# Late loads of x1 into the places of z2, and a reordered start and end of the second map

## The chip, the cores and the metric

The kernel runs on one core of a Trainium2 chip, all in fp32. The metric is the device time of one execution in microseconds; the figure quoted is the median of three. The engines in what follows are TensorE (PE, with its weight loads PEld), VectorE (DVE), ScalarE (ACT), GpSimd (POOL) and SyncE (SP), which here issues the loads and most stores by DMA; the stores of the output are issued by ACT.

## The reference

Two layers over x of shape (16, 1024, 256), each a residual around a normalised and rectified input. Cut to what matters:

```python
h = relu(layernorm(x))
# layer 0: graph weights from channel means, 4-head attention
g = relu(einsum('bcn,bnm->bcm', h_T, adj * A_s) * para)
x = x + softmax(q @ k.T * scale) @ v           # q from g, k and v from h @ kv_w
# layer 1
h = relu(layernorm(x))
agg = einsum('nm,bmd->bnd', A_hat, h)          # A_hat: adj + I, normalised by degree
z1 = agg @ W1.T + b1                           # 512 channels
z1 = relu(batchnorm(z1))                       # statistics over all 16 * 1024 rows
z2 = batchnorm(z1 @ W2.T + b2)                 # 256 channels, statistics over all rows
x = x + z2
```

The two batch norms need statistics over all rows, so the program has three stages: everything up to z1 for all batches, z2 for all batches, and the output for all batches.

## The kernel before

**Stage 1** (lines 171 to 1222) runs over 16 batches: layer norm, graph product, attention, layer norm, aggregation and first map. The result of layer 0, called x1, goes to device memory (`leave`, L943), and so does z1 in 32 tiles of 512 rows (two per batch). PSUM has three pools here: `ps_s` with three tiles of two banks, `ps_o` and `ps_t` with one bank each. They are all closed with the stage.

For the last two batches, 14 and 15, there is no further attention to hide behind. The code at L1176 to L1222 gives the aggregation of batch 14 (`linear1_all`, `linear1`, `linear1_seven`) three hooks, `first`, `second` and `third`, in which the second half of batch 15's attention output is scaled and added (`left[3]` to `left[5]`) and batch 15's second layer norm is made: `Norm.stats` (DVE, one `bn_stats` per 128 rows), `Norm.invert` (an add on DVE, then a power on POOL, L257), `Norm.shifts` (DVE, L263), `Norm.relu` (ACT, L278, eight rows of 256). `third` also transposes W2 through one tile of `ps_o` and one of `ps_t`. After the hook, `linear1_seven` adds two products to a tile of z1 (DVE, L864 and L865); then batch 15's aggregation starts (PE, L703). At its end (`very_last`) the last parts of z1 are made on PE (L891), evacuated by ACT (L900), their statistics taken by DVE, and the first rectified tiles of z1, zs[0,0] and zs[1,0], made by ACT (`relu_on`, L152).

**Stage 2** (L1241 to L1456) has its order written out by hand for all five engines. Tiles 0 and 1 (batch 0) are multiplied plainly (`plain`, `product`, L1255). The fourteen pairs of tiles of batches 1 to 14 are multiplied with seven products in place of eight (`Pair`: `m1` to `m7`, L1317; sums on DVE, L1307 to L1313). In one pass of the loop the products of one pair interleave with the rectification (ACT, L152) of the next pair and the copies `keep` (ACT, L1328) and adds `out` (DVE, L1331) that carry PSUM into `z2`. `z2` is one SBUF tile of [128, 2, 15, 1024]: two halves of the channels, 15 batches, 1024 rows, and is kept until stage 3. Tiles 30 and 31 (batch 15) come after the loop (L1476 to L1505): their results stay in four PSUM banks (`last`). PSUM pools are `ps_x` with four banks (the running sum `self.x` of a pair; later `last`) and `ps_z` with four (`begun`, `m2`, `m7`), which closes after the loop and makes room for `ps_out`, two tiles of two banks.

The last product, tile 31 for channel half 1, is split into two of 256 columns, so that the statistics of the first (L1496) run beside the second. `gather` makes the earlier tiles' statistics into triples; `bn2.invert` and `bn2.affine` end them.

**Stage 3** (L1538 to L1579) runs over the batches. PE transposes the scaled z2 into `ps_out` (L1534); `finish` scales z2 in place, two batches ahead, on ACT (L1514) or DVE (L1516); DVE adds the transposed result to x1 (L1573) in x1's tile; ACT issues the store (L1574).

x1 comes back from memory in half batches of 512 KB (`load_x1`, L1238). `AHEAD` is 10: batch 0 is loaded before the last pair, batches 1 to 6 and 9 in it and behind it, batches 7 and 8 into the places of the last z1 tiles, and batch b + 10 at the end of pass b of stage 3. These last six batches take tiles of the pool `io` (15 places of 4 KB per partition), in which the places are those of batches whose output has been stored. In front of batches 1 to 6 in SP's order stands the fetch of the last z1 tile, zs[31,2], into one of four places; the place before belonged to the last pair's b21, read by `m2`.

Of the kernel before, what the change touches and what calls it, by code (L numbers as in the profile page):

```python
# [29 lines left out]
def fast_path(  # L30
# [135 lines left out]
    def relu(t, f2):  # L166
        zs[t, f2] = fetch(t, f2)
        relu_on(zs[t, f2], f2)


    with ExitStack() as stage:
        ps_s = stage.enter_context(tc.tile_pool(name="fps_s", bufs=3, space=PSUM))
        ps_o = stage.enter_context(tc.tile_pool(name="fps_o", bufs=1, space=PSUM))
        ps_t = stage.enter_context(tc.tile_pool(name="fps_t", bufs=1, space=PSUM))
        big = stage.enter_context(tc.tile_pool(name="fbig", bufs=1))
# [870 lines left out]
        with tc.manual_schedule(engines={ENG.PE, ENG.Activation, ENG.DVE, ENG.Pool, ENG.SP}):  # L1046
# [73 lines left out]
            for b in range(B):  # L1120
# [55 lines left out]
                else:  # L1176
# [3 lines left out]
                    def first():  # L1180
                        norm.stats(0, 4)
                        left[3]()
                        left[4]()

                    def second():
                        pass

                    def third():
                        left[5]()
                        norm.stats(4, NC)  # L1190
                        norm.invert()
                        for n, (pool, tag) in enumerate(((ps_o, "o"), (ps_t, "t"))):
# [9 lines left out]
                            )  # L1202
                        norm.relu(0, NC)
                        leave(b)
# [20 lines left out]
    with ExitStack() as stage:  # L1225
# [5 lines left out]

        def load_x1(b, homes=None):

            xts[b] = []
            for h in range(NH):
                pool, tag, bufs = (homes or HOMES)[h]
                t = pool.tile([P, NC // NH, C], F32, tag=tag, name=f"f_x1t_{b}_{h}", bufs=bufs)
                nc.sync.dma_start(t, x1_d[b].rearrange("(p h i) d -> p h i d", h=NH, p=P)[:, h])  # L1238
                xts[b].append(t)

        st2 = big.tile([P, CC, TT, 6], F32, tag="st2", name="f_st2")  # L1241
        with tc.manual_schedule(engines={ENG.PE, ENG.Activation, ENG.DVE, ENG.Pool, ENG.SP}):
            bn1.affine(FC - 2, FC)

            z2 = big.tile([P, CC, B - 1, N], F32, tag="z2", name="f_z2")
            ps_x = stage.enter_context(tc.tile_pool(name="fps_x", bufs=4, space=PSUM))
            zps = ExitStack()
# [144 lines left out]
            pairs = {p: Pair(p) for p in SEVEN}  # L1392
            begun = {t: [bank(f"f_z2ps_{t}_{c}") for c in range(CC)] for t in (1, 0)}
            first = pairs[SEVEN[0]]
# [14 lines left out]
            first.m1()  # L1409
            first.keep(0, 0)  # L1410
            for p in SEVEN:
                now, soon = pairs[p], pairs.get(p + 1)
# [20 lines left out]
                if soon:  # L1433
                    soon.relu(1, 1)
                    soon.relu(1, 0)
                else:
                    relu_all(TT - 1)
                now.m5()
                now.keep(1, 1)
                if soon:  # L1440
                    soon.sums13()
                    soon.m1()
                    soon.keep(0, 0)
                now.out(1)
                now.m3()
# [13 lines left out]
            ps_out = stage.enter_context(tc.tile_pool(name="fps_out", bufs=2, space=PSUM))  # L1459
            last = {}  # L1460

            triples = big.tile([P, 6, 3], F32, tag="triples", name="f_triples")
            SPLIT = TT // 2
# [12 lines left out]
            for c in range(CC):  # L1476
                for t in range(TT - 2, TT):
                    ps = bank(f"f_z2ps_{t}_{c}", ps_x)
                    last[t % 2, c] = ps
                    if c + 1 < CC or t + 1 < TT:  # L1480
                        product(ps, t, c, 0)
                        product(ps, t, c, 2)
                        nc.vector.bn_stats(st2[:, c, t, :], ps)
                        continue
                    gather(1, SPLIT, TT - 1)
                    for k in range(2):
                        at = slice(256 * k, 256 * (k + 1))
                        for f in range(FC):
                            nc.tensor.matmul(
                                ps[:, at],  # L1490
                                w2T[:, f, ts(c, P)],
                                zs[t, f - f % 2][:, f % 2, at],
                                start=(f == 0),
                                stop=(f == FC - 1),
                            )
                        nc.vector.bn_stats(  # L1496
                            triples[:, 2 + 2 * k : 4 + 2 * k, :].rearrange("p k s -> p (k s)"),
                            ps[:, at],
                        )
                bn2.invert(  # L1500
                    c,
                    c + 1,
                    None if c + 1 < CC else triples.rearrange("p k s -> p (k s)"),
                )
                bn2.affine(c, c + 1)  # L1505
# [32 lines left out]
            for b in range(B):  # L1538
# [19 lines left out]
                else:  # L1558
                    for h in range(NH):
                        for c in range(CC):  # L1560
                            turn_out(b, h, c, outs[h])
                soon = [(b + 2, c) for c in range(CC) if (b + 2, c) not in ready]
                soon = soon if b + 2 < B else []
# [13 lines left out]
                finish_soon(False)  # L1577
                if b + AHEAD < B:
                    load_x1(b + AHEAD)  # L1579

# [513 lines left out]
```

## Time and profile before

| | us |
|---|---|
| median of three runs | 2431.84 (2431.0 to 2432.97) |
| the profiled execution | 2431.68 |
| its span, first to last instruction | 2429.8 |
| PE busy | 2387.0 (98%) |
| DVE busy | 1781.9 (73%) |
| ACT busy | 1325.6 (55%) |
| POOL busy | 308.2 (13%) |
| stage 2's first product starts | 2163.9 |
| first transpose into the output | 2362.9 |
| last store issued | 2420.6 |

Times on the profile's axis count from the first instruction, so the span ends at 2429.8. A busy share is an average over stages: PE's 98% hides that PE is at 100% in nearly all of stages 1 and 2 and about 60% in stage 3. The chain of work that ended last gives PE 96% and DMA 2% of the span.

### The profile page before, as it was taken

To read this page: it belongs to the slowest core of one execution; us is meant where nothing else is said; L and a number is where in the kernel's file an instruction comes from. 1 tells how busy PE (TensorE), PEld (TensorE's weight loads), DVE (VectorE), ACT (ScalarE), POOL (GpSimd) and SP (SyncE) were. 2 spreads that over 40 slices of the span, in tenths; PEclk is the share of its full clock that TensorE was granted. 3 is DMA by queue.
4 is the path that set the end of the run, shared out by engine and by line. 5 is a ranking of instruction groups with operands and counts; after the bars stand their busy time and mean duration, and the time that the engine had idled before them with its cause. 6 is when DMAs were issued, how large, how long until landed. Compare 5 with 4: busy or idle time off the path is not lost.

```text
span 2429.8 us, 24669 instructions
## 1 busy us (share of the span) xinstructions
PE 2387.0 (98%) x8042; PEld 1053.3 (43%) x8042; DVE 1781.9 (73%) x2441; ACT 1325.6 (55%) x1932; POOL 308.2 (13%) x546
## 2 busy tenths in 40 slices
PE   8999999999999999999999999999999999999995
PEld 4453444434343434444343434344443434444444
DVE  6878677685949586776859595867768596757766
ACT  6845555464636455554546364545545465346653
POOL 2030202020020302020201103020202010000000
PEclk9999999999999999999999999999999999999997
DMA  5041414232331415142323224141423212355569
GB/s 186 9 140 61 152 61 126 87 91 73 116 94 60 144 61 152 61 126 87 102 67 114 91 63 142 61 151 61 126 87 110 67 61 76 110 209 178 174 225 379
DMA packets 176634, 275.77 MB, mean 113 GB/s; under 512 B 37872, under 2 KB 121328, under 8 KB 176496
## 3 DMA queue, kind: packets, MB, share of 16 engines
q1 hardware_dynamic: 156336, 241.55, 30.6%
q0 software_dynamic: 15552, 15.77, 2.5%
q10 hardware_dynamic: 4608, 16.78, 1.7%
q8 instruction: 66, 1.08, 0.2%
q14 instruction: 72, 0.59, 0.1%
HBM read 169.35 MB, written 71.10 MB: 99 GB/s over the span
## 4 chain that ended last, share of the span: by engine, by line
PE 96%; DMA 2%; DVE 1%; ACT 0%; issue 0%; SPq 0%; POOL 0%; DVEq 0%; ACTq 0%; POOLq 0%
PE f_s L506 19%; PE f_o L547 18%; PE f_gps L398 18%; PE f_aps L703 16%; PE f_zps L809 6%; PE f_vps L423 5%; PE f_zx L1317 4%; PE f_zm L1317 3%; PE f_kpsx L467 2%; PE f_kps L467 1%; DMA out_dram<-f_x1t 1%; PE f_z2ps L1255 1%; PE f_zps L891 1%; PE f_kps L440 1%; PE f_zps3a L809 0%; PE f_zps3b L809 0%
## 5 line engine op out<-in xcount | busy, mean ns | idle before, releaser
L514 ACT ACTIVATE f_p<-f_s 128x1024 f32<-128x1024 f32 x512 | 477.3, 1048 | 150.2 <-PE f_s L506 150.1
L523 DVE TENSOR_TENSOR f_acc<-f_acc,f_p 128x1024 f32<-128x1024 f32 x384 | 470.5, 1225 | 41.1 <-ACT f_w L345 0.5
L506 PE MATMUL f_s<-f_qT,f_kT 64*128 64x512 f32 x2048 | 456.8, 596 | 0.0
L547 PE MATMUL f_o<-f_p,f_v 128*64 128x512 f32 x2048 | 453.6, 595 | 0.0
L398 PE MATMUL f_gps<-f_w,f_h_a 128*128 128x512 f32 x1024 | 444.7, 594 | 0.3 <-DVE f_w L336 0.3
L368 POOL DMA_DIRECT2D f_hT<-f_hQ x480 | 235.8, 499 | 1220.0 <-PE f_gps L398 1170.8
L506 PEld LDWEIGHTS f_s<-f_qT,f_kT 64*128 64x128 f32 x2048 | 190.8, 186 | 263.5 <-ACT f_p L514 117.0
L398 PEld LDWEIGHTS f_gps<-f_w,f_h_a 128*128 128x128 f32 x1024 | 192.8, 190 | 247.0 <-issue 230.7
L547 PEld LDWEIGHTS f_o<-f_p,f_v 128*64 128x64 f32 x2048 | 141.4, 137 | 304.3 <-issue 254.4
L349 DVE SCALAR_TENSOR_TENSOR f_w<-f_w,f_adj 128x1024 f32<-128x1024 f32 x127 | 153.9, 1212 | 38.8 <-ACT f_w L348 38.8
L345 ACT ACTIVATE f_w<-f_row,f_col 128x1024 f32<-128x1024 f32 x127 | 147.0, 1158 | 31.2 <-DMA f_row<-frow 30.2
L278 ACT ACTIVATE f_h_b<-f_x,f_shift_b,f_rstd_b 128x256 f32<-128x256 f32 x128 | 67.8, 594 | 160.9 <-DVE f_shift_b L263 160.9
L348 ACT ACTIVATE f_w<-f_w 128x1024 f32<-128x1024 f32 x127 | 134.3, 1058 | 4.0
L703 PE MATMUL f_aps<-f_ahatT,f_hs 128*128 128x512 f32 x256 | 115.1, 592 | 0.0
L703 PE MATMUL f_aps<-f_ahatT,f_h_b 128*128 128x512 f32 x256 | 112.7, 593 | 0.8 <-DVE f_z L865 0.8
L423 PE MATMUL f_vps<-f_kvw,f_hT 128*128 128x256 f32 x512 | 113.4, 379 | 0.0
L703 PE MATMUL f_aps<-f_t,f_hs 128*128 128x512 f32 x256 | 112.5, 592 | 0.0
L278 ACT ACTIVATE f_h_a<-f_x,f_shift_a,f_rstd_a 128x256 f32<-128x256 f32 x126 | 73.8, 587 | 63.5 <-DVE f_shift_a L263 63.4
L423 PEld LDWEIGHTS f_vps<-f_kvw,f_hT 128*128 128x128 f32 x512 | 97.2, 190 | 20.3 <-issue 7.4
L520 DVE TENSOR_TENSOR f_acc<-f_p,f_p 128x1024 f32<-128x1024 f32 x64 | 76.3, 1192 | 15.3 <-ACT f_p L514 15.3
L589 ACT COPY f_recs<-f_rec 32x32 f32<-32x32 f32 x128 | 31.5, 246 | 98.7 <-DVE f_rec L581 97.5
L574 ACT COPY f_parts<-f_red 32x64 f32<-32x64 f32 x128 | 39.1, 306 | 78.5 <-DVE f_red L539 77.4
(227 smaller groups left out, 2709.7 us busy)
## 6 DMA issues: line engine op xcount, KB each, us to landing
f_t<-ft SPq DMA_DIRECT2D x84, 512.0 KB, 6.9
fz<-f_z SPq DMA_DIRECT2D x64, 512.0 KB, 9.6
f_x<-in_x_dram SPq DMA_DIRECT2D x31, 1024.0 KB, 8.1
f_zb<-fz SPq DMA_DIRECT2D x42, 512.0 KB, 4.3
f_para<-in_L_gnn_para_dram SPq DMA_DIRECT2D x32, 512.0 KB, 4.5
f_att<-f_oT SPq DMA_DIRECT2D x512, 32.0 KB, 1.9
fx<-f_x SPq DMA_DIRECT2D x16, 1024.0 KB, 6.3
f_x1t<-fx SPq DMA_DIRECT2D x32, 512.0 KB, 7.3
```

What stands on the lines that cost most here:

```text
L345: nc.scalar.activation(w, rows[b], AF.Abs, bias=cols[b][:, c : c + 1], scale=0.5 / C)
L349: nc.vector.scalar_tensor_tensor(w, w, 1.0, adj_t[c], ALU.subtract, ALU.mult)
L368: queue.dma_start(to[ts(k, 32), ts(a, 32 * NC)], t[ts(a, 32), k].rearrange("i c r -> i (c r)"),)
L398: nc.tensor.matmul(gps[d][:, ts(g, 512)], hs[b][:, c, ts(d, P)], w[:, ts(g, 512)], start=(c == 0), stop=(c == NC - 1),)
L423: nc.tensor.matmul(ps[:, i, :], hT[e][:, ts(c4 + i, P)], kvw_t[:, e, C : 2 * C], start=(e == 0), stop=(e == CC - 1),)
L506: nc.tensor.matmul(ps[:, e, :], kT[rows_e, pair, ts(m, P)], qT[rows_e, pair, ts(g, 512)], start=True, stop=True,)
L514: nc.scalar.activation(p, ps, AF.Exp)
L523: nc.vector.tensor_add(acc_of[s], acc_of[s], p)
L547: nc.tensor.matmul(o_of[s][e * HD : (e + 1) * HD, :], v[:, m, ts(2 * pair + e, HD)], p[:, e, :], start=(m == 0), stop=(m == NC - 1),)
L703: nc.tensor.matmul(ps, left[:, m, :], right(m), start=not more and m == 0, stop=(m == KH - 1), skip_group_check=more,)
L809: nc.tensor.matmul(ps[i], left[:, ts(i, P)], right, start=not more, stop=True, skip_group_check=more,)
L1317: nc.tensor.matmul(ps, left[:, m, :], right[:, m, :], start=start and m == 0, stop=(m == 1), skip_group_check=not start,)
```

## The change

It has five parts.

1. The pools `ps_o` and `ps_t` are opened ahead of stage 1 and stay open to the end. `ps_x` has two banks in place of four. Tiles 0's two products (`begun[0]`) go to one tile of each of these pools (`aside`), and later the products of tiles 30 and 31 for channel half 0 (`ends`).
2. Batch 15's second layer norm is made in two halves: statistics and power of rows 0 to 3 in `first`, their shifts and rectification in `second`, and the other half in `third`.
3. In the last pass over the pairs, the rectification of tile 31 moves from in front of `m5` to behind `keep(1, 1)`, and the product of tile 30 for channel half 0 follows it, in front of `m3`.
4. The last product is no longer split; its statistics are one `bn_stats` over 512 columns, and `triples` has four entries in place of six.
5. The loads of batches 10 to 15 go into `z2[:, h, b, :]`, the places of batch b's two channel halves, and are issued behind the transposes of batch b in place of the end of pass b.

```diff
+    ps_o = ctx.enter_context(tc.tile_pool(name="fps_o", bufs=1, space=PSUM))
+    ps_t = ctx.enter_context(tc.tile_pool(name="fps_t", bufs=1, space=PSUM))
     with ExitStack() as stage:
         ps_s = stage.enter_context(tc.tile_pool(name="fps_s", bufs=3, space=PSUM))
-        ps_o = stage.enter_context(tc.tile_pool(name="fps_o", bufs=1, space=PSUM))
-        ps_t = stage.enter_context(tc.tile_pool(name="fps_t", bufs=1, space=PSUM))
...
                     def first():
                         norm.stats(0, 4)
+                        norm.invert(0, 4)
                         left[3]()
                         left[4]()
                     def second():
-                        pass
+                        norm.shifts(0, 4)
+                        norm.relu(0, 4, False)
                     def third():
                         left[5]()
                         norm.stats(4, NC)
-                        norm.invert()
+                        norm.invert(4, NC)
...
-                        norm.relu(0, NC)
+                        norm.shifts(4, NC)
+                        norm.relu(4, NC, False)
                         leave(b)
...
-        def load_x1(b, homes=None):
+        def load_x1(b, homes=None, places=None):
...
+                if places is not None:
+                    t = places[h].rearrange("p (i d) -> p i d", d=C)
+                else:
...
-            ps_x = stage.enter_context(tc.tile_pool(name="fps_x", bufs=4, space=PSUM))
+            ps_x = stage.enter_context(tc.tile_pool(name="fps_x", bufs=2, space=PSUM))
...
-            begun = {t: [bank(f"f_z2ps_{t}_{c}") for c in range(CC)] for t in (1, 0)}
+            def aside(name):
+                return [
+                    ps_o.tile([P, 512], F32, tag="o", name=f"{name}_0"),
+                    ps_t.tile([P, 512], F32, tag="t", name=f"{name}_1"),
+                ]
+            begun = {0: aside("f_z2ps_0"), 1: [bank(f"f_z2ps_1_{c}") for c in range(CC)]}
...
+            def last_product(t, c, ps):
+                last[t % 2, c] = ps
+                for f2 in range(0, FC, 2):
+                    product(ps, t, c, f2)
...
-                else:
-                    relu_all(TT - 1)
                 now.m5()
                 now.keep(1, 1)
                 if soon:
                     soon.sums13()
                     soon.m1()
                     soon.keep(0, 0)
+                else:
+                    relu_all(TT - 1)
+                    ends = aside("f_z2ps_end")
+                    last_product(TT - 2, 0, ends[0])
                 now.out(1)
                 now.m3()
...
-            triples = big.tile([P, 6, 3], F32, tag="triples", name="f_triples")
+            triples = big.tile([P, 4, 3], F32, tag="triples", name="f_triples")
...
-                    ps = bank(f"f_z2ps_{t}_{c}", ps_x)
-                    last[t % 2, c] = ps
+                    if (t % 2, c) not in last:
+                        last_product(t, c, ends[1] if c == 0 else bank(f"f_z2ps_{t}_1", ps_x))
                     if c + 1 < CC or t + 1 < TT:
-                        product(ps, t, c, 0)
-                        product(ps, t, c, 2)
-                        nc.vector.bn_stats(st2[:, c, t, :], ps)
+                        nc.vector.bn_stats(st2[:, c, t, :], last[t % 2, c])
                         continue
                     gather(1, SPLIT, TT - 1)
-                    for k in range(2):
...
+                    nc.vector.bn_stats(
+                        triples[:, 2:4, :].rearrange("p k s -> p (k s)"), last[t % 2, c]
+                    )
...
                             turn_out(b, h, c, outs[h])
+                if b + AHEAD < B:
+                    load_x1(b + AHEAD, places=[z2[:, h, b, :] for h in range(NH)])
...
                 finish_soon(False)
-                if b + AHEAD < B:
-                    load_x1(b + AHEAD)
```

More of the change, by code (lines that the diff above doesn't have):

```diff
@@ L1230, in fast_path @@
         HOMES = [(io, "x1", None)] * NH
-        def load_x1(b, homes=None):
+        def load_x1(b, homes=None, places=None):
             xts[b] = []
             for h in range(NH):
-                pool, tag, bufs = (homes or HOMES)[h]
-                t = pool.tile([P, NC // NH, C], F32, tag=tag, name=f"f_x1t_{b}_{h}", bufs=bufs)
+                if places is not None:
+                    t = places[h].rearrange("p (i d) -> p i d", d=C)
+                else:
+                    pool, tag, bufs = (homes or HOMES)[h]
+                    t = pool.tile(
+                        [P, NC // NH, C], F32, tag=tag, name=f"f_x1t_{b}_{h}", bufs=bufs
+                    )
                 nc.sync.dma_start(t, x1_d[b].rearrange("(p h i) d -> p h i d", h=NH, p=P)[:, h])
@@ L1410, in fast_path @@
             first.keep(0, 0)
+            last = {}
+            def last_product(t, c, ps):
+                last[t % 2, c] = ps
+                for f2 in range(0, FC, 2):
+                    product(ps, t, c, f2)
             for p in SEVEN:
@@ L1459, in fast_path @@
             ps_out = stage.enter_context(tc.tile_pool(name="fps_out", bufs=2, space=PSUM))
-            last = {}
-            triples = big.tile([P, 6, 3], F32, tag="triples", name="f_triples")
+            triples = big.tile([P, 4, 3], F32, tag="triples", name="f_triples")
             SPLIT = TT // 2
@@ L1477, in fast_path @@
                 for t in range(TT - 2, TT):
-                    ps = bank(f"f_z2ps_{t}_{c}", ps_x)
-                    last[t % 2, c] = ps
+                    if (t % 2, c) not in last:
+                        last_product(t, c, ends[1] if c == 0 else bank(f"f_z2ps_{t}_1", ps_x))
                     if c + 1 < CC or t + 1 < TT:
-                        product(ps, t, c, 0)
-                        product(ps, t, c, 2)
-                        nc.vector.bn_stats(st2[:, c, t, :], ps)
+                        nc.vector.bn_stats(st2[:, c, t, :], last[t % 2, c])
                         continue
                     gather(1, SPLIT, TT - 1)
-                    for k in range(2):
[L1487 to L1499, printed above, removed]
+                    nc.vector.bn_stats(
+                        triples[:, 2:4, :].rearrange("p k s -> p (k s)"), last[t % 2, c]
+                    )
                 bn2.invert(
```

## The prediction

> **What bounds the kernel now.** I read the table of stretches first, because the page's slices are too coarse for the last 100 us, where most edits lie. Columns: stretch, length, busy us of PE, weight loads, DVE, ACT and POOL with instruction counts, granted TensorE clock, DMA share, GB/s.
>
> ```profile
> 2332.00:2338.00 6.00, 6.00 (x15) 2.66 (x14) 4.89 (x7) 4.00 (x6) 0.00 (x0) 1.00 0.01 3
> 2338.00:2342.00 4.00, 4.00 (x10) 1.71 (x9) 1.98 (x4) 2.00 (x3) 0.00 (x0) 1.00 0.67 179
> 2342.00:2362.00 20.00, 17.71 (x47) 8.57 (x46) 8.88 (x21) 6.09 (x8) 0.55 (x1) 1.00 1.01 396
> 2362.00:2374.00 12.00, 8.87 (x64) 7.03 (x64) 9.48 (x15) 6.68 (x6) 0.55 (x1) 1.00 0.77 270
> 2374.00:2404.00 30.00, 18.17 (x112) 15.00 (x111) 18.93 (x18) 12.67 (x11) 0.00 (x0) 0.78 1.02 413
> 2404.00:2424.00 20.00, 13.08 (x89) 11.08 (x88) 15.47 (x14) 7.97 (x9) 0.00 (x0) 0.84 1.03 417
> ```
>
> Two regimes. Until about 2342 PE has no gap worth the name (the stretches before are at 100% too). From 2342 to 2424 the DMA engines are full at 396 to 417 GB/s, except from 2362 to 2374, at 270. So the tail ends when about 33 MB (30 half loads of x1, one of z1, 32 half stores, 0.52 MB each) have been moved, counted from 2338, when the first of them is issued. Only three things shorten this kernel: an earlier 2338, fewer holes after it, or an earlier end of PE's stages, which is an earlier 2338.
>
> Next the waits. Of the DMA queue on SP from 2366 to 2400, and of PE's longest pauses around the last linear stage (2110 to 2125, 2160 to 2178) and the last pair (2336 to 2368). Columns: waiter, releaser, total us, times, longest.
>
> ```profile
> SPq L1238 <- DMA out_dram<-f_x1t: 30.5, 12, 7.2
> ```
>
> ```profile
> DVE f_shift_b L263 <- POOL f_rstd_b L257: 1.8, 1, 1.8
> ...
> PE f_aps L703 <- DVE f_z L865: 0.8, 1, 0.8
> ```
>
> ```profile
> PE f_z2ps L1255 <- ACT f_z L900: 1.4, 1, 1.4
> ```
>
> ```profile
> PE f_zx L1317 <- ACT f_z L1328: 1.8, 1, 1.8
> ACT f_z L152 <- DMA f_z<-fz: 1.1, 1, 1.1
> ```
>
> All twelve late loads of x1 wait for stores to land; PE pauses for 0.83, 1.40 and 1.77 us. Last, POOL's powers by shape:
>
> ```profile
> L257 POOL TENSOR_TENSOR f_rstd_b<-f_var_b,f_mhalf 128x8 f32<-128x8 f32 x16 | 27.5, 1721 | 149.1 <-DVE f_var_b L256 149.1
> L257 POOL TENSOR_TENSOR f_rstd_a<-f_var_a,f_mhalf 128x4 f32<-128x4 f32 x2 | 2.1, 1055 | 2.3 <-DVE f_var_a L256 2.3
> ```
>
> **What the Trainium skill says.** "DMA: Bandwidth & Descriptors", section "Bandwidth", puts the ceiling of the core's port fabric at 435 GB/s; the trace's plateau of 413 to 417 GB/s is 95% of it, so I treat the plateau as a limit that reordering can't raise. The same page, "Queues, rings and completion order", says each DMA engine takes turns between the queues that have work. The trace agrees: from 2384 to 2400 the stores' queue moved 3.54 MB and the loads' 3.16 MB. "TensorE: Matmul & The Clock Gate", Part 1, says a PE with too little to do falls to half clock; the trace shows 0.78 granted in 2374 to 2404. "PSUM — Partial Sum Buffer", "Specifications", gives 8 banks of 512 fp32 values, which is how I count the pools below.
>
> **The change, part by part.** Its own profile: span 2429.8, time 2431.68, 1.9 around it; the median shown is 2431.84, 0.16 above. I work with differences and take them from the median.
>
> *Half norms of the last batch.* The 8-column power, its statistics' tail and eight ACT rows become two halves. In the third hook DVE stands at L263 for POOL (power 2120.05 to 2121.69), with L864 and L865 (1.22 us each) behind it in order; L865 frees the PSUM tile for which PE waits, from 2123.66 to 2124.49. With four columns the power takes 1.05 instead of 1.64: L865 ends 0.59 sooner, PE starts at 2123.90. Gain 0.59 of 0.83. Added: one variance add and one shift on DVE (0.17 each) in the hooks before, under waits of 2.73 and 3.4 us; one power on a POOL that is otherwise idle; four of ACT's eight relus (8 took 4.04) now at 2101.4 to 2103.4, before L755, for which ACT stands idle until 2103.94. If that cover failed, L755 would slip by at most 2 us, and DVE and PE slots behind it with it. Bounds for the part: 0.2 to 0.83; I take 0.59.
>
> *PSUM pools o and t live on; the first z2 products go there.* PE ended f_zps at 2162.50 and began f_z2ps at 2163.90, released by ACT's last evacuation L900 (2163.17 to 2163.86). By the banks, 2 (o, t) + 2 (ps_x) + 4 (ps_z) = 8, the new homes have had no user since about 2129, so only the relu of zs[0,0] is left, which ended at 2162.60. Gain 1.26. The next wait is for the second relus: they depend on ACT and DVE, which do not move; PE would want zs[0,2] at 2169.5 and ACT had it at 2169.42. In the first pair ACT is busy until 2178.5; keep(0,0) would then end near 2179.1, and m6 wants it at 2179.8; keep(0,1) near 2182.5 and m5 at 2183.2. Tight by 0.6 us, but covered. ps_x with 2 buffers holds the two f_zx alive at a time. Bounds: 0 (if the wait is of another tile) to 1.4; I take 1.26.
>
> Both gains are PE's and pass through the thirteen following pairs (2177.7 to 2338, PE 100%) to SP: the fetch of zs[31,2], for which PE's m2 frees a slot at 2337.9, heads SP's queue of loads. So 2338 comes 1.85 us earlier.
>
> *The last pair.* relu_all(31) moves behind keep(1,1), and a product of tile 30 (four matmuls, 3.43 us) in front of m3. The 1.77 us pause goes, since keep(1,1) no longer stands behind two relus that await a DMA landing at 2342.67; the unsplit last product drops the 0.52 pause at L1489 and 0.2 of split cost, for 0.27 more of statistics (0.70 for 0.43). Relative to m2: m5 ends 2342.9, then 3.43 + 1.72 + 1.72 + 10.30 gives 2360.05 for PE, last statistics 2360.3 to 2361.0 against 2363.54: 2.5 us sooner. Behind it, unchanged, 1.5 us of aggregation, scaling, transposes, add: the first store issues at 2365.1 instead of 2367.66. m3 and m4 come 1.7 us later in PE's time, and they free two of the loads' places, at 2348.1 and 2349.9; those loads were issued at 2349.41 and 2351.97, so nothing slips. By itself all this moves no DMA byte: it counts in the next sum.
>
> *Loads into z2 behind the transposes.* Twelve half loads no longer wait for a store to land (7 to 10 us after its issue) but for eight transposes (1.1 us). SP has nothing queued behind them. The hole: 12 us at 270 and the rest at 381 until 2378 lacks, against 418, (418−270)×12 + (418−381)×4 = 1.92 MB, or 4.6 us. In the new order the loads of batches 7 and 8 are issued at 2355.2 to 2360.3 (they were at 2357.2, 2358.9, 2362.3, 2363.1, behind PE's reads of z), which keeps the engines full to about 2366; stores from 2365.1 and loads from 2366.3 show about 1.2 us later. Hole left: about 0.3. Gain 4.3; bounds 2.5 (the new loads gain nothing, only stores and four loads come sooner) to 4.6.
>
> Does the tail then stay DMA bound? Loads and stores share until about 2397, then some 19 stores are left, 19 × 1.25 = 24 us. DVE needs per batch two adds of 1.22 and on average 0.4 of scaling, 2.85 us, ACT about 2.5, against 2.5 for the DMA; but by then the chain is up to eight stores ahead. Eight batches × 2.85 from 2397 end near 2420 at worst, the DMA near 2422. Covered, by 2 us.
>
> Sum: 0.59 + 1.26 + 4.3 = 6.15 us. 2431.84 − 6.15 = **2425.7 us**, −0.25%.
>
> **Rivals.**
> A. The new places bring nothing: the load's wait turns out to be for more than the batch's transposes (the scaling of later batches in the same z2, or a landing as before). For it: z2 is one tile. Against: reads, copies and statistics of z2 overlap in the trace at 2343 to 2352. Then 1.85 + about 2 = 3.9 us: 2428.0.
> B. The wait at 2163.9 only changes its name (relu, or ACT in the first pair, where cover is 0.6 us). For it: ACT is 8.87 of 10 us busy at 2170 to 2180. Then 0.59 + 4.3: 2426.95, on the bound.
> C. Loads ahead of stores starve the end. Loads taken early leave more stores than now for the last stretch; if loads got well over the half that they get now, the stores would begin in earnest only at 2381 (12 × 1.25 after 2366), PE at half clock, where 32 transposes took 6.33 us (2402.2), 3.2 per batch, and the add of 1.22 not overlapped: 4.4 × 14 batches = 62, end 2443; plus 3 of landing, 2.5 of close and 1.9 around the span, less 1.85 and 0.3: about 2448. It decides once a batch takes over 3.6 us from 2381 on (50 us in place of 62). Against it: the equal shares above, and four stores in flight per side.
>
> **How the numbers follow.** 0.2%, 4.9 us, is about what a measurement of this kernel can tell from none: 2426.98. Forecast 62%, A 17%, B 13%, C 8%. The forecast's own range, with the three gains at 0.2 to 0.83, 0.6 to 1.4 and 3.4 to 4.6 (their lower ends are B and A), is 2425.0 to 2427.6; A and B stretch the upper end, repeat spread (1 us either way) both: 2424.0 to 2428.6. Faster: the forecast less a tenth (56%), half of B and a fifth of A: 66%. Same: 26%. Slower: C, 8%.
>
> **What would show it.** Right: PE's pause before f_aps near 0.2, before f_z2ps under 0.2, none before m3; DMA at or above 395 GB/s in every stretch from first load to last store; the late loads issued 1 us behind transposes, all by about 2390 instead of 2398. Wrong: a new pause of PE in the first pair (B), SP waiting for landings (A), or a DMA share under 0.95 after the last load (C).

## The result and the profile after

The changed kernel takes 2425.47 us (median of ten runs, 2424.30 to 2427.18) against 2432.19 us for the kernel before (median of ten), a ratio of 0.9972 with a 95% interval of 0.9964 to 0.9980: 6.7 us, or 0.28%, faster. The forecast was 2425.7. The profiled execution has a span of 2424.1 us and a time of 2425.91, 5.77 below the profiled execution of before.

Every line number from 170 on has moved: L257 is now L258, L703 is L704, L1238 is L1247, L1255 is L1264, L1317 is L1326, L1328 is L1337, L1514 and L1516 are L1526 and L1528, L1534 is L1546, L1574 is L1588.

First the table of stretches, with the same columns as before (stretch, length, busy us and instructions of PE, weight loads, DVE, ACT and POOL, granted clock, DMA share, GB/s):

```profile
2330.00:2336.00 6.00, 6.00 (x15) 2.66 (x14) 4.89 (x7) 3.96 (x6) 0.00 (x0) 1.00 0.01 3
2336.00:2340.00 4.00, 4.00 (x10) 1.71 (x9) 1.16 (x2) 0.59 (x1) 0.00 (x0) 1.00 0.94 228
2340.00:2360.00 20.00, 18.27 (x49) 8.35 (x47) 10.25 (x28) 8.96 (x11) 1.10 (x2) 1.00 1.02 407
2360.00:2372.00 12.00, 9.85 (x56) 8.83 (x57) 9.35 (x10) 6.80 (x7) 0.00 (x0) 0.72 1.01 377
2372.00:2384.00 12.00, 6.23 (x48) 5.14 (x48) 9.41 (x9) 2.05 (x2) 0.00 (x0) 1.00 1.03 416
2384.00:2396.00 12.00, 8.48 (x48) 7.24 (x48) 6.12 (x6) 7.55 (x7) 0.00 (x0) 0.72 1.03 398
2396.00:2402.00 6.00, 4.26 (x32) 3.43 (x32) 5.83 (x7) 4.68 (x5) 0.00 (x0) 1.00 1.03 421
```

The stretch around the first stores, 270 GB/s before, is at 377. A smaller hole is left in it, and there is a new dip, 398, from 2384 to 2396. Next the waits of SP's queue from 2358 to 2400 (waiter, releaser, total us, times, longest):

```profile
SPq L1247 <- PE f_outps L1546: 7.0, 5, 3.2
SPq L1247 <- DMA out_dram<-f_x1t: 5.5, 2, 3.0
SPq L1247 <- DMA f_z<-fx: 5.1, 3, 2.1
```

Before, all twelve late loads waited for a landing of a store, 30.5 us in all. Now five waits end with the transposes (L1546); two are still put down to a store and three to an earlier late load, for a reason that the last section gives. Then PE's timeline at the three places where it used to pause (start, duration, instruction, count; a pause would stand in brackets at the end of the line):

```profile
2122.26 1.02 PE L810 MATMUL f_zps3b<-f_aggT,f_w1s 128*128 128x512 f32 x2
2123.32 1.98 PE L704 MATMUL f_aps<-f_ahatT,f_h_b 128*128 128x512 f32 x4
```

```profile
2147.45 13.90 PE L892 MATMUL f_zps<-f_aggT,f_w1T 128*128 128x512 f32 x32
2161.19 13.90 PE L1264 MATMUL f_z2ps<-f_z,f_w2T 128*128 128x512 f32 x32
```

```profile
2338.35 1.88 PE L1326 MATMUL f_zx<-f_zb,f_w2s 128*128 128x512 f32 x4
2340.06 3.60 PE L1264 MATMUL f_z2ps_end<-f_z,f_w2T 128*128 128x512 f32 x8
2343.50 1.88 PE L1326 MATMUL f_zx<-f_zb,f_w2s 128*128 128x512 f32 x4
```

All three pauses (0.83, 1.40, 1.77 us) are gone: each line starts as the one above it ends. In the third fence the product of tile 30 stands where the pause was. POOL's power and DVE's wait for it from 2090 to 2125 are these two rows, of the groups and of the waits:

```profile
L258 POOL TENSOR_TENSOR f_rstd_b<-f_var_b,f_mhalf 128x4 f32<-128x4 f32 x2 | 2.0, 1006 | 102.8 <-DVE f_var_b L257 102.8
```

```profile
DVE f_shift_b L264 <- POOL f_rstd_b L258: 1.1, 1, 1.1
```

One wait of 1.8 us has become one of 1.1; the other half's power lies beside other work.

**How the two traces are compared.** Profiled executions differ in when they reach batch 14's `f_zps`: at 2109.57 to 2111.85 us over the fourteen traces here, although ahead of it the edits add only the first half of a norm, beside other work. Spans compared as they stand carry up to 2 us of that. Cut at events, the traces repeat to 0.03 in the first two rows of the table below, to 0.4 from there to the fetch, and to about 1 in what follows, for kernels with the same code there. The table gives the lengths in us, from PE's products `f_zps` of batch 14 (2110.61 in before) to the end of the span. The other columns are experiments that are described below.

| from, to | before | changed | e3 norm halves alone | e4 PSUM homes alone | e1 late loads alone | e2 without late loads | e5 without pair order |
|---|---|---|---|---|---|---|---|
| `f_zps`, `f_aps` | 13.89 | 13.09 | 13.10 | 13.88 | 13.88 | 13.09 | 13.09 |
| `f_aps`, `f_z2ps` | 39.41 | 37.87 | 39.44 | 37.84 | 39.41 | 37.87 | 37.87 |
| `f_z2ps`, fetch of zs[31,2] | 174.07 | 173.96 | 174.06 | 174.23 | 174.06 | 173.96 | 174.25 |
| fetch, first store | 29.69 | 27.08 | 29.10 | 29.27 | 29.27 | 27.08 | 28.99 |
| first store, end of span | 62.15 | 61.88 | 63.12 | 62.95 | 62.01 | 63.93 | 61.09 |
| last two together | 91.84 | 88.96 | 92.22 | 92.22 | 91.28 | 91.01 | 90.08 |

From before to changed, PE's stages are shorter by 0.80 + 1.54 + 0.11 = 2.45 us and the end, from the fetch on, by 2.88. That makes 5.33; the remaining 0.4 of the spans' 5.7 is the time at which `f_zps` is reached. Where several executions show the same end, I use their mean. For the old order of the end these are before, e3 and e4: 92.1. For the new order they are the changed kernel, e8, e9 and e11: 88.9. The end is 3.2 us shorter.

One more thing is to be kept in mind: a trace shows one execution, and not the median one. The profiled executions of the old order (before, e3, e4) took 0.25 us less than the medians of their kernels on average, those of the new order (changed, e8, e9, e11) 0.5 us more. So the traces, taken together, show the change some 0.75 us smaller than the medians do.

### The profile page after: what moved, and what is told of

Read it like the earlier page. It is cut to its first block, busy times and chain, and to the rows that moved or that the text cites. A ratio compares the mean times of both kernels' runs of the same rounds, so it can differ in the third digit from the quotient of the medians.

```text
span 2424.1 us, 24651 instructions
## 1 busy us (share of the span) xinstructions
PE 2384.8 (98%) x8034; PEld 1050.7 (43%) x8034; DVE 1781.2 (73%) x2442; ACT 1325.8 (55%) x1932; POOL 308.6 (13%) x547
## 4 chain that ended last, share of the span: by engine, by line
PE 93%; DVE 3%; DMA 2%; issue 1%; SPq 1%; POOL 0%; ACT 0%; DVEq 0%; ACTq 0%; POOLq 0%
PE f_s L507 17%; PE f_o L548 17%; PE f_gps L399 17%; PE f_aps L704 16%; PE f_zps L810 6%; PE f_vps L424 4%; PE f_zx L1326 4%; PE f_zm L1326 3%; PE f_kpsx L468 2%; PE f_kps L468 1%; DVE f_acc L524 1%; PE f_outps L1546 1%; PE f_z2ps L1264 1%; PE f_kps L441 1%; PE f_zps L892 1%
## 5 line engine op out<-in xcount | busy, mean ns | idle before, releaser
L704 PE MATMUL f_aps<-f_ahatT,f_hs 128*128 128x512 f32 x256 | 115.1, 592 | 0.0
L704 PE MATMUL f_aps<-f_ahatT,f_h_b 128*128 128x512 f32 x256 | 112.7, 593 | 0.0
L704 PE MATMUL f_aps<-f_t,f_hs 128*128 128x512 f32 x256 | 112.5, 592 | 0.0
```

Of the source, the lines that this page charges most:

```text
L704: nc.tensor.matmul(ps, left[:, m, :], right(m), start=not more and m == 0, stop=(m == KH - 1), skip_group_check=more,)
```

## The experiments

The kernel before was timed again beside each experiment, on the same chip. The ratios' intervals are about 0.2% wide; sizes of single parts therefore rest on the traces' lengths too, and where the two disagree I say so.

**e1, the late loads alone.** Before, with the loads of batches 10 to 15 in z2's places, behind the transposes.

```diff
+                if b + AHEAD < B:
+                    load_x1(b + AHEAD, places=[z2[:, h, b, :] for h in range(NH)])
                 soon = [(b + 2, c) for c in range(CC) if (b + 2, c) not in ready]
...
-                if b + AHEAD < B:
-                    load_x1(b + AHEAD)
```

> The kernel before with part 5 alone: batches 10 to 15 loaded into the places of z2 behind the transposes; PSUM pools, norm halves, last pair and split last product as before. Theory 1 (the tail is a fixed number of bytes behind a fixed start): the stage starts as before, the first store is issued near 2367.7, and the hole from 2362 to about 2368 stays because nothing is there to load; only its second part, 2368 to 2378, is filled, (418-294)x2 + (418-397)x2 + (418-253)x2 + (418-380)x4 over 418, that is 1.8 us: -1.8 us, between -1 and -2.5. Theory 2 (rival A of the prediction, the places bring nothing): 0 within 0.5 us, and SP still waits for stores. Theory 3 (most of the whole gain is this part): -4 us or more.

Measured: 2430.22 against 2432.06, ratio 0.9995 (0.9986 to 1.0003), so 1.8 us by the medians, as Theory 1 had it, and by the traces 0.8 (92.1 to 91.3). Neither size is clear of noise by itself.

**e2, everything but the late loads.** The changed kernel with those loads back in `io`'s places at the end of the pass (the reverse of the diff above).

> The changed kernel without part 5: batches 10 to 15 again into the pool's places, when a store has landed. Theory 1: the earlier start (1.9 by the prediction, 2.8 by the profile of the changed kernel) and the earlier first store and four loads stay; the hole is filled in part: -4 to -5 us against before, so part 5 is worth about 2 us in this setting. Theory 2: as the changed kernel, -6.5 us. Theory 3: -2 us.

Measured: 2428.11 against 2432.06, ratio 0.9984 (0.9977 to 0.9991), 3.95 us faster than before. The table shows where the earlier first store goes: fetch to first store is as short as in the changed kernel (27.08), but first store to end is 63.93 in place of 61.88. The late loads bring the changed kernel 2.6 us by the medians and 2.1 by the traces. The stretches of e2 around its first stores:

```profile
2362.00:2366.00 4.00, 3.41 (x17) 3.37 (x18) 2.89 (x3) 1.91 (x2) 0.00 (x0) 0.57 0.79 312
2366.00:2370.00 4.00, 3.36 (x27) 2.65 (x27) 3.84 (x4) 1.70 (x2) 0.00 (x0) 1.00 0.79 214
2370.00:2374.00 4.00, 3.02 (x24) 2.36 (x22) 3.88 (x5) 2.38 (x2) 0.00 (x0) 1.00 1.01 412
2374.00:2382.00 8.00, 5.32 (x40) 4.25 (x41) 7.25 (x8) 3.62 (x3) 0.00 (x0) 1.00 1.03 387
```

and of the changed kernel:

```profile
2362.00:2366.00 4.00, 3.75 (x18) 3.75 (x19) 2.59 (x4) 2.26 (x2) 0.00 (x0) 0.50 1.02 396
2366.00:2370.00 4.00, 3.80 (x24) 3.35 (x22) 3.51 (x4) 1.36 (x2) 0.00 (x0) 0.75 0.96 321
2370.00:2374.00 4.00, 3.11 (x25) 2.57 (x24) 3.88 (x5) 2.38 (x2) 0.00 (x0) 1.00 1.02 412
2374.00:2382.00 8.00, 4.25 (x34) 3.44 (x32) 5.76 (x7) 1.24 (x1) 0.00 (x0) 1.00 1.03 419
```

In e2 the DMA engines stand idle a fifth of the time (share 0.79) from 2362 to 2370; in the changed kernel they do not. Counted against 418 GB/s over these 20 us, e2 lacks 1.51 MB or 3.6 us, the changed kernel 0.49 MB or 1.2 us.

**e3, the halves of the norm alone**, in before:

```diff
                     def first():
                         norm.stats(0, 4)
+                        norm.invert(0, 4)
...
                     def second():
-                        pass
+                        norm.shifts(0, 4)
+                        norm.relu(0, 4, False)
...
-                        norm.invert()
+                        norm.invert(4, NC)
...
-                        norm.relu(0, NC)
+                        norm.shifts(4, NC)
+                        norm.relu(4, NC, False)
```

> The kernel before with part 2 alone, the last layer norm in halves. Theory 1: PE's pause before f_aps falls from 0.83 to about 0.2 us or to nothing, and the whole program shifts: -0.6 to -0.8 us. Rival: other work of ACT or DVE takes the place of the wait (the four early relus delay L755), or the gain is eaten at the next wait, before f_z2ps: 0, or a loss of up to 1 us.

Measured: 2431.47 against 2432.06, ratio 0.9995 (0.9987 to 1.0004). The median difference is 0.59, too small to be told from none by itself; the trace has it at its place. The first two lines are PE's timeline at `f_aps`, where the pause is gone; the last is PE's wait ahead of `f_z2ps`, which stays:

```profile
2122.41 1.02 PE L809 MATMUL f_zps3b<-f_aggT,f_w1s 128*128 128x512 f32 x2
2123.47 1.98 PE L703 MATMUL f_aps<-f_ahatT,f_h_b 128*128 128x512 f32 x4
```

```profile
PE f_z2ps L1258 <- ACT f_z L900: 1.4, 1, 1.4
```

`f_zps` to `f_aps` is 0.79 shorter, and up to the fetch nothing later grows for it.

**e4, the PSUM homes alone**: in before, `ps_o` and `ps_t` stay open and take `begun[0]` and, after the loop, the ends; `ps_x` has two banks; order and split as before.

```diff
+            begun = {0: aside("f_z2ps_0"), 1: [bank(f"f_z2ps_1_{c}") for c in range(CC)]}
...
+            ends = aside("f_z2ps_end")
...
-                    ps = bank(f"f_z2ps_{t}_{c}", ps_x)
+                    ps = ends[t % 2] if c == 0 else bank(f"f_z2ps_{t}_{c}", ps_x)
```

> The kernel before with part 1 alone: pools o and t live on, ps_x has two banks, tile 0's products and later those of tiles 30 and 31 for half 0 in o and t; order of the last pair and split last product as before. Theory 1: PE goes from f_zps to f_z2ps without the pause of 1.40 us, the first pairs keep up, and the load of zs[31,2] comes by that much earlier: -1.3 to -1.6 us. Rival B of the prediction: the pause moves to a relu or into the first pair: 0 to -0.5 us, with a new pause of PE between 2163 and 2190.

Measured: 2430.72 against 2432.06, ratio 0.9992 (0.9984 to 1.0). Here the pause of 0.83 stays and that of 1.40 goes, in the waits and in PE's timeline:

```profile
PE f_aps L704 <- DVE f_z L866: 0.8, 1, 0.8
```

```profile
2148.53 13.90 PE L892 MATMUL f_zps<-f_aggT,f_w1T 128*128 128x512 f32 x32
2162.26 13.90 PE L1256 MATMUL f_z2ps<-f_z,f_w2T 128*128 128x512 f32 x32
```

No pause of PE is listed in its place in the first pair, so rival B is out: `f_aps` to `f_z2ps` is 1.57 shorter, and `f_z2ps` to fetch 0.16 longer, no more than that length varies between kernels with the same code there (173.96 to 174.33).

**e5, the changed kernel without the new order of the last pair**: the rectification of tile 31 back in front of `m5`, the product of tile 30 behind the loop; the last product stays whole.

```diff
+                else:
+                    relu_all(TT - 1)
                 now.m5()
...
-                else:
-                    relu_all(TT - 1)
-                    ends = aside("f_z2ps_end")
-                    last_product(TT - 2, 0, ends[0])
```

> The changed kernel with part 3 undone: in the last pass tile 31 is rectified in front of m5 again and tile 30's product comes after the loop. Theory 1: the pause of PE in front of m3 is back (1.3 to 1.8 us), the last statistics, the first store and the last of the four loads of batches 7 and 8 come that much later, and so a hole of 1 to 2 us reopens ahead of the stores: -5 to -5.5 us against before, where the whole change gave -6.7. Theory 2 (the tail is DMA bound and PE's order no longer counts): as the changed kernel, -6.5 to -7.

Measured: 2428.63 against 2432.43, ratio 0.9985 (0.9978 to 0.9991). Fetch to first store is 28.99, 1.9 more than with the order, nearly all of it one pause in PE's waits:

```profile
PE f_zx L1326 <- ACT f_z L1337: 1.6, 1, 1.6
```

Without the order the kernel is 3.2 us slower than the changed one by the medians, more than Theory 1 gave it, and by the traces' ends 1.2 (90.1 against 88.9). Its trace, whose execution took just the median time, reaches `f_zps` 1.3 us later than the changed kernel's (2111.50 and 2110.22), which no edit explains. Its stretches from 2362 to 2382 lack 1.56 MB, or 3.7 us. The size is thus known only as 1.2 to 3.2.

Part 4, the last product in one piece, was not tried apart. e5 has it and the old order, and its fetch to first store is 28.99, against 29.10 and 29.27 in e3 and e4 without it; so it is worth a few tenths of a us at that place at most, by these traces.

**e6, the late loads left out.** Batches 10 to 15 add what lies in z2's places, so their output is not x1 + z2, and 6.3 MB of loads are missing.

```diff
-                    load_x1(b + AHEAD, places=[z2[:, h, b, :] for h in range(NH)])
+                    xts[b + AHEAD] = [
+                        z2[:, h, b, :].rearrange("p (i d) -> p i d", d=C) for h in range(NH)
+                    ]
```

> The changed kernel with the loads of batches 10 to 15 left out: their adds use what lies in z2's places, so their outputs are not x1 plus z2; 6.3 MB fewer are moved. Theory 1 (bytes): 12 x 0.524 MB at 418 GB/s is 15.0 us, less the slow start of the loads, until the chain of DVE and ACT is the limit: 32 adds of 1.22 and 6.5 scalings of 0.81 from 2361 end at 2405, the last landing 3 us later near 2408, against 2422: -14 to -15 us against the changed kernel, about -21 against before. If the chain is slower than the sum of DVE's durations (PE at half clock, 3.2 us per batch and more), less: -8 us against the changed kernel, -15 against before; then the cover that the prediction gave the last stretch (2 us) was too large.

Measured: 2414.44 against 2432.43, ratio 0.9928 (0.9913 to 0.9944), 11 us below the changed kernel, and by the ends in the traces 12.1 (76.8 against 88.9). That lies between the two theories, nearer to the first: its chain was to end at 2405, and the last store is issued at 2404.2. The stretches, and the stores by their tiles (duration in ns, first and last issue, and the time from issue to landing):

```profile
2372.00:2400.00 28.00, 21.99 (x168) 17.77 (x167) 27.28 (x26) 18.51 (x17) 0.00 (x0) 1.00 0.96 384
```

```profile
L1590 ACTq DMA_DIRECT2D out_dram<-f_x1t x20: 338/338/483, 2362.0 to 2388.2; - x20
L1590 ACTq DMA_DIRECT2D out_dram<-f_z x12: 338/338/339, 2389.6 to 2404.2; - x12
DMA to landing us min/median/max: 2.6/3.7/5.3
```

DVE is busy 27.28 of 28 us while 384 GB/s are moved: freed of the loads, the end is bound by the chain of transposes, scaling and adds, at (2404.2 − 2362.0) / 31 = 1.36 us per store, 2.7 per batch. The last store can then be issued 9.5 us sooner than in the changed kernel (2413.7), and the last landing comes 13 us sooner after the first store (46.73 in place of 59.77). So the changed kernel's end is bound by bytes and not by this chain. PE's lower clock in the table of stretches (0.72) is not tried by e6, where the clock is 1.00; that it costs nothing is read from the DMA engines, which are at a share of 1.01 to 1.03 in those stretches. Rival C needed more than 3.6 us per batch.

**e7, three of the loads ahead of the fetch.** In the changed kernel the DMA engines stand nearly idle (3 GB/s) from 2330 to 2336, since all loads of x1 but batch 0's stand behind the fetch of zs[31,2] in SP's order. Here batches 1 to 3 go in front of it.

```diff
+                    for n in range(1, 4):
+                        load_x1(n)
                     zs[TT - 1, 2] = fetch(TT - 1, 2)
-                    for n in range(1, AHEAD - 3):
+                    for n in range(4, AHEAD - 3):
```

> The changed kernel with the loads of batches 1 to 3 in front of the fetch of zs[31,2] in SP's order; their places are free up to 4 us before that of zs[31,2]. Theory 1: the DMA engines, idle from 2330 to 2335 in the changed kernel, move up to six half loads there, but the loads that can be made before the stage's end are limited by places, so the engines run dry before the first store at 2362 instead: what is gained is the part of the loads' slow start that moves into idle time, and nothing else: -0.5 to -1.5 us against the changed kernel. Theory 2 (a fixed number of bytes behind a start, with no limit by places): the start is 4 to 6 us earlier, so -4 to -6. Rival: the fetch now waits behind loads in the queue, relu of tile 31 comes late and PE waits in front of tile 31's product: 0 to +2.

Measured: 2425.37 against 2432.43, ratio 0.9971 (0.9960 to 0.9982): the changed kernel's time, 0.1 below its median, where Theory 1 had at least 0.5.

```profile
2328.00:2340.00 12.00, 12.00 (x29) 5.32 (x28) 9.17 (x11) 7.28 (x11) 0.00 (x0) 1.00 1.01 393
2340.00:2364.00 24.00, 21.24 (x61) 9.96 (x59) 11.63 (x30) 10.59 (x12) 1.10 (x2) 1.00 0.81 276
```

The idle stretch is used at 393 GB/s, and the next 24 us then run at 276, because no place is free for another load: from 2325 to 2400 SP waits for PE's reads of z for 8.5 and 8.0 us, and for the transposes for 9.6. Bytes moved early are worth something here only if other bytes can follow at once.

**e8 and e9, the position of the late loads in the code.** In e8 the changed kernel has the call at the end of the pass:

```diff
-                if b + AHEAD < B:
-                    load_x1(b + AHEAD, places=[z2[:, h, b, :] for h in range(NH)])
...
                 finish_soon(False)
+                if b + AHEAD < B:
+                    load_x1(b + AHEAD, places=[z2[:, h, b, :] for h in range(NH)])
```

e9 puts the load of batch b + 8 at pass b, so the same places are used two passes later in SP's order.

```diff
-                if b + AHEAD < B:
-                    load_x1(b + AHEAD, places=[z2[:, h, b, :] for h in range(NH)])
+                if 2 <= b < 8:
+                    load_x1(b + 8, places=[z2[:, h, b - 2, :] for h in range(NH)])
```

> The changed kernel with the late loads in the places of z2, but in the order at the end of pass b, where they stood before. Theory 1: SP has nothing else to do, so only the place counts and not the position: as the changed kernel within 0.7 us, -6 to -7 against before. Rival: the position sets which earlier DMA a load or a store has to wait for, so stores begin or end elsewhere: a difference of over 1 us.

> The changed kernel with the late loads held back by two passes: batch b + 8 goes into the places of batch b - 2 at pass b, for b from 2 to 7, so the first of them is issued some 5 us after the first stores instead of 4 us before. Theory 1 (the loads' early start fills the hole ahead of and beside the first stores): the engines run at what the stores alone bring, about 385 GB/s or 320 to 345 in the first 8 us as in the run without late loads, where the changed kernel had 411 to 340: +0.5 to +1.5 us against the changed kernel. Theory 2 (early late loads slow the first stores, so that ACT stands for a landing, 2.6 us at 2368 in the changed kernel): -0.5 to -1.

Measured: e8 2425.57 against 2432.43, ratio 0.9972 (0.9961 to 0.9983); e9 2425.15 against 2432.23, ratio 0.9971 (0.9960 to 0.9983). As a test of timing both edits were misses, and that tells something. SP's issue of the twelve loads in the changed kernel and, below it, in e9 (start, length until the last, count):

```profile
2358.52 24.45 SPq L1247 DMA_DIRECT2D f_z<-fx  x12
```

```profile
2358.81 24.15 SPq L1247 DMA_DIRECT2D f_z<-fx  x12
```

SP has nothing else to do there: it stands at the first load until the place is free, wherever the load stands in its order. What the change bought is the place, not the position. The Trainium skill, "DMA: Bandwidth & Descriptors", in "Anatomy of one DMA — SWDGE (gpsimd) path", says that any semaphore wait of a DMA happens on the issuing sequencer ahead of dispatch; these two runs on SP's queue agree (2358.52 and 2358.81).

**e10 and e11.** e10 is e7 and e9 together; e11 is the changed kernel once more, beside them.

> Both edits: the loads of batches 1 to 3 in front of the fetch of zs[31,2], and the late loads held back by two passes. If the end is set by the first store and the bytes that are still to be moved behind it: as the kernel with held loads alone, within 0.7 us. If it is set by the start of the stream of loads: at least 3 us faster than that.

> The changed kernel once more, on the same chip as the two with held loads: 0.9972 of the time before, within 0.0006, for a comparison of small differences.

Measured: 2425.20 and 2425.40 against 2432.23, ratios 0.9971 (0.9960 to 0.9982) and 0.9972 (0.9961 to 0.9983). By the traces the end from the fetch on is 1.2 us shorter with the loads ahead of the fetch (87.7 in e7 and e10 against 88.9); the medians show at most 0.2. I can't call it a gain.

**e12, later places.** As e9, but batch b + 8 goes into batch b's places, two batches' work later. The loads now really come later.

```diff
-                    load_x1(b + 8, places=[z2[:, h, b - 2, :] for h in range(NH)])
+                    load_x1(b + 8, places=[z2[:, h, b, :] for h in range(NH)])
```

> The changed kernel with batch b + 8 loaded into the places of batch b, for b from 2 to 7: each late load now waits for transposes that come two passes later, so the first is issued after the first stores, near 5 us behind the first instead of 3.7 us before it. The two kernels that were to hold the loads did not: SP waits for the place alone, so a later position in the program moved nothing, and their times are the changed kernel's. Theory 1 (the first store and the bytes still to be moved behind it set the end): the stores alone bring 320 to 385 GB/s in the first 6 us, where the changed kernel had 411 to 327: within 1 us of the changed kernel, -6 to -7 against before. Theory 2 (it is the loads' early issue that brings the part of 2.8 us): back to the time without part 5, -4. Theory 3 (early late loads cost more, by stores and ACT standing for landings, than they fill): -7.5 or better.

Measured: 2427.51 against 2432.13, ratio 0.9981 (0.9974 to 0.9988), 2.1 us slower than the changed kernel (2425.40 in e11, same chip): most of what leaving out the new places costs (e2, 2.6). By the end in the trace it is 0.7 (89.6 against 88.9); the traced execution took 0.8 us less than e12's median. SP's timeline and the stretches of e12:

```profile
2366.53 22.76 SPq L1247 DMA_DIRECT2D f_z<-fx  x12
```

```profile
2362.00:2366.00 4.00, 3.54 (x26) 2.84 (x27) 3.90 (x5) 2.31 (x2) 0.00 (x0) 1.00 0.78 309
2366.00:2370.00 4.00, 3.01 (x24) 2.30 (x22) 4.00 (x5) 2.81 (x4) 0.00 (x0) 1.00 1.04 303
2370.00:2374.00 4.00, 3.58 (x28) 2.98 (x29) 3.88 (x4) 0.88 (x1) 0.00 (x0) 1.00 0.91 310
2374.00:2382.00 8.00, 2.83 (x17) 2.60 (x16) 2.66 (x4) 1.24 (x1) 0.00 (x0) 0.69 1.01 408
```

By the medians Theory 1, which had e12 within 1 us of the changed kernel, has failed, and the 4.6 us gained on before lie near the 4 of Theory 2. Waits for stores are not the reason, as SP's waits for its late loads end with PE, 18.3 us, and with earlier loads, 6.0. So most of the gain comes from the loads being there between the last of the early loads and the flow of stores, from 2358 on, and not from 2366 on.

## Why the prediction held

**The halves of the norm, 0.59.** Right in kind, a little small: 0.80 by the changed kernel's trace, 0.79 in e3's. The wait for POOL fell by 0.7 (1.8 to 1.1), in part because the power took 1.006 us where 1.055 was used, and a pause of 0.24 that was left standing in the sum is not there. The four relus at 2100.9 cost nothing, as argued.

**The PSUM homes, 1.26.** 1.54 by the trace, 1.57 in e4's, 1.34 by e4's median. All of the 1.40 pause went. The working had kept 0.14 of it, until the second of zs[0,0]'s two relus ends; in the changed trace the two run from 2159.93 to 2161.45 and PE starts at 2161.19, ahead of the second one's end. The cover of 0.6 us in the first pair held: PE has no wait there.

**The last pair, first store 2.5 sooner relative to `m2`.** Fetch to first store is 2.6 shorter than in before's trace and 2.0 to 2.2 shorter than in e1, e3 and e4, whose pause at that place was 1.2 to 1.3 in place of 1.77. The statement that this moves no byte by itself was right in part: in e2 the stretch behind the first store grew by 1.8 of these 2.6 us (62.15 to 63.93), and the end as a whole became 1.1 shorter. Two figures in this part of the working are not what the lines show. The 1.5 us from the last statistics to the first store are 4.1 in before (2363.53 to 2367.66), and 4.1 is also what its own times give (2361.0 and 2365.1). And the stores' 7 to 10 us to landing hold only from the fifth store on; the first four landed 3.0 to 5.7 us after their issue. Neither enters the sum.

**The hole, 4.3.** This is the term that the traces show to be mis-sized: the end is 3.2 us shorter, not 4.3. Against 418 GB/s, from 2362 to 2382 (2360 to 2380 in e1, which is earlier), the bytes lacking are in the table below. For before they follow from the 270 GB/s up to 2374, in the prediction's table, and this line:

```profile
2374.00:2382.00 8.00, 5.96 (x47) 4.76 (x45) 7.88 (x8) 3.62 (x3) 0.00 (x0) 1.00 1.02 397
```

| | MB lacking | us lacking |
|---|---|---|
| before | 1.94 | 4.6 |
| e1, late loads alone | 1.64 | 3.9 |
| e2, all but the late loads | 1.51 | 3.6 |
| e5, all but the pair's order | 1.56 | 3.7 |
| e12, late loads from 2366 on | 1.41 | 3.4 |
| changed | 0.49 | 1.2 |

The hole left is 1.2 us and not about 0.3, and the changed kernel has a second one of 0.6 (355 GB/s from 2386 to 2390). 4.6 − 1.2 − 0.6 = 2.8, near the 3.2. The stretch from 2366 to 2370, at 321, also breaks the condition that every stretch would hold 395. That the time came out right nevertheless has two reasons: the two PE terms were 0.5 larger than forecast, and the medians differ by about 1 us more than the traces' lengths add up to (2.4 + 3.2 = 5.6 against 6.7). Of that 1 us some 0.75 is the choice of executions named above. In which stretch it lies the runs don't show; were all of it in the end, the end's gain would be 4.3 after all. The interval of the ratio (4.9 to 8.8 us) holds both. That the forecast time is only 0.2 off is luck in another way too: 6.15 us were forecast and 6.7 measured, but the median of before, 2431.84 of three runs, became 2432.19 of ten.

The table also shows what the sum did not say: the parts help one another. Late loads alone close 0.7 us of the hole, all the rest without them 1.0, both together 3.4 (2.8 with the second hole). The ends say the same, 0.8 and 1.1 against 3.2, though single ones repeat to about 1 us only. With the late loads alone the flow is at 292 to 330 GB/s for 12 us (2360 to 2372 in e1), with early stores alone at 312 and 214 for 8; with both it is at 396 and 321. So it was better to put everything into one term for the hole than to add up single parts.

**When the late loads go out.** They were expected from about 2364.5 (2366.3 less 1.85) to 2390; they went out from 2358.52 to 2382.65. The first load went out as soon as the transposes of channel half 0 of batch 0 were done, 3.7 us ahead of the first store, and the second 0.7 us ahead of it; the working had put both behind it. This is part of the gain, as e12 shows.

**The cover at the end, 2 us.** Far too small an estimate, though it was named as the worst case: 11 us by the medians and 13 by the last landing (e6). The working took 2.85 us per batch, and e6 shows 2.7; the error was to start the chain's count only where the loads end.

**The rivals.** A gave 2428.0 for places that bring nothing; e2, which takes them out, has 2428.11. The estimate was good, and its premise false, since the places brought 2.6. B is refuted by e4 and by the lack of any listed pause in the first pair, C by e6's 2.7 us per batch and by the 415 to 421 GB/s that the changed kernel holds from 2390 to 2410, where C had the stores starved.

**The picture of the whole.** That the tail ends when about 33 MB have been moved, counted from 2338, was too simple. e7 moves 4.7 MB in 2328 to 2340 and gains nothing that the medians can tell. What counts is when the first store goes out, how many bytes are then still to be moved, and whether loads and stores together keep the engines full from there on. The plateau itself held: 407 to 421 GB/s in the stretches without a dip, under the 435 that the Trainium skill, "DMA: Bandwidth & Descriptors", "Bandwidth", gives as the ceiling of the port fabric.

## What to carry to other kernels

Where the end of a kernel is bound by bytes, look for a buffer that dies early and give it to the loads: in this kernel not the position of a load in its queue decided when it was issued, but the moment at which its place came free. Then count the DMAs in flight, as here no more than eight were (next section). An earlier first store and earlier loads each closed little of the hole in the DMA flow as long as the other was missing, so try them together before either is dropped. Compare traces by the lengths between events and not by their spans, when the expected gain is a few microseconds of 2400.

## What the runs showed of the hardware

- Full engines that move less. In the changed kernel from 2366 to 2370, and in e12 over the same stretch, the DMA share is 0.96 and 1.04 at 321 and 303 GB/s, against 1.02 at 412 from 2370 to 2374 in the changed kernel. A share near 1 is thus no proof that the plateau's bytes are moved. Both lie where the stores begin beside the loads; the cause wasn't found.
- A store can stand behind a load that it does not use, because at most eight of these DMAs are in flight. From 2378 to 2386 ACT's timeline in the changed kernel (start, duration or time until the last of the group, instruction, pause and its releaser) is:

```profile
2380.13 5.43 ACTq L1588 DMA_DIRECT2D out_dram<-f_x1t  x2
2385.61 1.24 ACT L1526 ACTIVATE f_z<-f_z,f_bn_t,f_bn_s 128x1024 f32<-128x1024 f32 x1 [6.10 <-DMA f_z<-fx]
```

  The second of the two stores is issued at 2385.22; it stores a batch that has its own x1 tile, and the profile names the landing of a late load as releaser. The trace also holds the semaphore that each DMA raises when it lands. From 2358 on SP's loads and ACT's stores share eight of them, in turn, and ahead of 43 of the 44 DMAs there in the changed kernel the issuing engine waits for the same semaphore. The store at 2385.22 has the semaphore of the load issued at 2373.39, which landed at 2385.14; the store at 2380.13 has that of a load which landed at 2380.06. In none of the fourteen traces is a DMA issued there before the earlier one on its semaphore has landed, and never are more than eight in flight. Five of the twelve late loads of the changed kernel, all from 2372.97 on, go out within 0.1 us of such a landing, two of a store and three of a load. ACT, which also scales z2, stands meanwhile, and the 355 GB/s from 2386 to 2390 follow; in e8 a store is held in the same way, for 4.0 us, and the stretch is at 414, so the hold alone doesn't make the dip. How much time the eight semaphores cost was not tried.
- Loads issued early wait in flight in place of SP: from issue to landing the twelve late loads take 10.4 us in the changed kernel (median) and 7.2 in before, the stores 8.3 against 7.2. The hole closed although each transfer took longer.
